# Five edits to a two-layer graph network: the sort's operands in PSUM, one-hots on ScalarE, more routing buffers, no second residual array, result sums on TensorE

## The chip, the cores and the metric

The kernel runs on one core of a Trainium2 chip. The metric is the device time of one execution in microseconds (us), as the median of several runs. The engines are TensorE (PE, with PEld for its weight loads), VectorE (DVE), ScalarE (ACT), GpSimd (POOL) and SyncE (SP). SBUF and PSUM are the on-chip memories of 128 partitions; PSUM takes the results of matmuls.

## What is computed

A graph network of two layers on 6250 nodes of 256 features and 100000 edges, all in fp32. Cut to what matters:

```python
# layer 0
xn = _layernorm(x)
agg = segment_sum(edge_weight[:, None] * xn[src], dst, N)         # GNN
x = x + relu(agg @ W + b) + linear_attention(xn)                  # 8 heads
x = x + expert(argmax(router(_layernorm(x))))                     # 32 experts, top 1
# layer 1
xn = _layernorm(x)
h = (xn @ W).reshape(n, 4, 64)
e = leaky_relu((a_l * h).sum(-1)[src] + (a_r * h).sum(-1)[dst])   # row = src, col = dst
att = exp(e - segment_max(e, src)[src]) / segment_sum(...)[src]
x = x + segment_sum(att * h[dst], src) + galerkin_attention(xn)   # 8 heads
xn = _layernorm(x)
vals, idx = top_k(xn @ gate_w + gate_b, 2)                        # 16 experts, top 2
y = xn + sum(softmax(vals) * expert[idx](xn))
x = x + (y - mean(y)) / sqrt(var(y) + 1e-5) * gamma + beta
```

The edges come sorted by `dst`. Layer 1 needs them sorted by `src`, so the kernel sorts 131072 keys itself.

## The kernel before

Nodes are taken in 49 tiles (NT) of 128, a node a partition. The program is one stream of stages; the times are those of the profiled execution.

**Layer 0, edge loop (126 to 1376 us, L825 to L850).** 196 groups (QA) of four tiles of 128 edges. For each tile POOL issues an indirect DMA that gathers 128 rows (`gather`, L300, `xg<-xw_d,idx`, 782 in all), DVE builds a weighted one-hot matrix S (L836), and PE multiplies it with the rows into the PSUM tile `ps` (L839, four tiles added up; one matmul is two records in the profile). `ps` has three buffers of [128, 256] fp32. Two DVE additions per group (L842) put it where its nodes lie in `agg`. `xg` has six buffers. Between the groups two generators are advanced by a list of due points (L844): `beside`, the linear attention of layer 0, in 99 steps from group 0 to 116, its first half the k and v of each tile (kv steps), its second half the queries and outputs (q steps); and `order`, the sort, its part 1 in 55 steps from group 4 to 116 and its part 2 in 98 steps from group 116 to 192. The scheduler may move these instructions from where they are written; it hasn't a schedule written out by hand here.

**The sort (`edge_order`, L497 to L607).** A bitonic sort of [128, 1024] keys. One step is two DVE instructions, a minimum (L526) and a maximum (L527) of two halves. Part 1 (`step`) sorts within a partition, SBUF to SBUF in the tile `o_x`. Then `banks()` runs `beside` to its end and opens a PSUM pool, since part 2 needs PE transposes (`turned`, L563). After a transpose the keys stand in PSUM (`o_t`); ACT copies one half to SBUF (`o_e`, L588, or `o_z`, L598), and DVE compares PSUM with SBUF. All the other steps of part 2 compare SBUF with SBUF.

**Layer 0 routing and experts, and rows of layer 1 (1376 to 1843).** The routing (`dispatch`, L345 to L495) serves both layers. For groups of `bt` tiles, `logits` makes the layernorm into `xn` and the router's logits, and `put` chooses experts, finds the places of the tokens and scatters the rows (POOL, L442, `f_xs<-xn,d_pi`). The logits of the next group are written ahead of the `put` of the present one.

**Layer 1, attention loop (1843 to 3143).** 25 chunks of up to 32 tiles of edges, in an order written out by hand (`manual_schedule`, L1556 to L1573), three chunks in flight: `loads`; `weigh` (DVE scans for the running maximum, and ACT's exponentials, L1474); `own_part`; `gain` (rows times weights, L1515; a copy by ACT, L1517; one-hots S, L1520; matmuls, L1525); `rows_to` (32 gathers, L300, `h<-h_d,idx`); `own_logits`. The last makes, in steps of eight tiles, a transposed one-hot ST: the row numbers, broadcast from DRAM, are compared with the partition's number in place (DVE, L1378, 128x1024), and PE multiplies with it (L1383).

**Layer 1 routing (3156 to 3380).** `dispatch` in groups of four tiles, with `finals` (L1872) in front: it reads the layer's input `xs1_d` into `xl`, adds the attention, and stores the sum as `xs2_d`.

**Layer 1 experts (3380 to 3782).** PE is busy 398 of 402 us. Beside it `with_beta` (L1914) loads `xs2_d` in seven pieces, adds beta and stores it again. The biases `b2` lie in the memory of `acc`, which is no longer needed.

**Tail (3782 to 3892, L2004 to L2018).** Seven groups of seven tiles: load the two expert results `xc` and `yg` and the residual `xe`, add the two (DVE, L2011), layernorm (L119 statistics, L124 normalisation), times gamma (L2014), plus `xe` (L2015), store.

Of the kernel before, what the change touches and what calls it, by code (L numbers as in the profile page):

```python
# [8 lines left out]
F32 = mybir.dt.float32  # L9
# [11 lines left out]
P = 128  # L21
# [5 lines left out]
CH = 7  # L27
# [25 lines left out]
def gps_kernel(ctx, tc, x, src, dst, edge_weight, g0_W, g0_b, m0_WqT, m0_WkvT, m0_WpT, m0_bp,  # L53
# [12 lines left out]
                   allow_small_or_imprecise_dtypes=True)  # L66
    ident = cst.tile([P, P], F32, name="ident")
# [277 lines left out]
    def dispatch(name, fb, fw, pps, ne, nk, bt, rw, rb, ns, xs_d, finals):  # L345
# [19 lines left out]
        def logits(t0):  # L365
            n = min(bt, NT - t0)
            x_ = finals(t0, n)
            xn = [fw.tile([P, bt, rw_], F32, name=f"xn{k}", bufs=3) for k in range(nk)]
            layernorm(fw, x_, xn[0][:, :, :C], n)
            for k in range(nk):  # L370
                if k:
                    nc.scalar.copy(xn[k][:, :n, :C], xn[0][:, :n, :C])
                nc.vector.tensor_copy(xn[k].bitcast(I32)[:, :n, C], ids[:, k, t0:t0 + n])
                if nk == 2:
                    nc.vector.memset(xn[k][:, :, C + 2], 1.0 - k)
            lp = pps.tile([P, bt, ne], F32, name="lp")
            for i in range(n):
                xT = transposed(fw, pps, xn[0][:, i, :C], "xT")
                for c in range(2):
                    nc.tensor.matmul(lp[:, i, :], xT[:, c, :], rw[:, c, :], start=c == 0, stop=c == 1)  # L380
            lg = fw.tile([P, bt, ne], F32, name="lg")
            nc.vector.tensor_tensor(lg[:, :n, :], lp[:, :n, :],
                                    rb[:, None, :].to_broadcast([P, n, ne]), op=OP.add)
            return xn, lg

        def put(t0, xn, lg, turn):
            n = min(bt, NT - t0)
            ti = fw.tile([P, bt, 8], U32, name="ti")
# [59 lines left out]
        held = logits(0)  # L448
        for j, t0 in enumerate(range(0, NT, bt)):
            ahead = logits(t0 + bt) if t0 + bt < NT else None  # L450
            put(t0, *held, j % 2)
            held = ahead
# [44 lines left out]
    def edge_order(pool, tmp, out, banks):  # L497
# [31 lines left out]
        def step(x, h, flip=False):  # L529

            y = tmp.tile([P, SC], F32, name="o_x")
            pairs(*halves(x, h), *halves(y, h), flip)
            return y
# [24 lines left out]

        def turned(x, i):

            p = pps.tile([P, SH], F32, name=f"o_t{i}")
            for b in range(SH // P):
                nc.tensor.transpose(p[:, b * P:(b + 1) * P],  # L563
                                    x[:, i * SH + b * P:i * SH + (b + 1) * P], ident)
            return p

        half = [slice(i * SH, (i + 1) * SH) for i in range(2)]
        for k in range(7):
            y, z = (tmp.tile([P, SC], F32, name="o_x") for _ in range(2))
            t = [None, None]  # L570
            for i in sides:
                if k:
                    pairs(*halves(x[:, half[i]], 1), *halves(z[:, half[i]], 1))
                    signed(z, y, k + 1, half[i])
                else:
                    signed(x, y, k + 1, half[i])
                t[i] = turned(y, i)
            yield

            for j in reversed(range(k + 1)):  # L580
                y = tmp.tile([P, SC], F32, name="o_x")
                for i in sides:
                    v = t[i].rearrange("p (n two h) -> p n two h", two=2, h=1 << j)
                    a, b = v[:, :, 0, :], v[:, :, 1, :]
                    if j == k:
                        e = pool.tile([P, SH // 2], F32, name="o_e", bufs=2)
                        e = e.rearrange("p (n h) -> p n h", h=1 << j)
                        nc.scalar.copy(e, b)  # L588
                        b = e
                    pairs(a, b, *halves(y[:, half[i]], 1 << j))  # L590
                    t[i] = y[:, half[i]]
                yield
# [7 lines left out]
            x = tmp.tile([P, SC], F32, name="o_x")  # L600
            pairs(p[0], e, x[:, half[0]], x[:, half[1]])
            yield
            for j in reversed(range(1, 9)):
                x = step(x, 1 << j)
                yield
        x = step(x, 1)
# [46 lines left out]
    with tc.tile_pool(name="l0", bufs=1) as lp:  # L653
# [87 lines left out]
        with tc.tile_pool(name="g0w", bufs=4) as gw, tc.tile_pool(name="e0", bufs=1) as ep, \  # L741
                tc.tile_pool(name="e0t", bufs=3) as et, \
                tc.tile_pool(name="g0p", bufs=3, space=PSUM) as gps:
# [71 lines left out]
            late = ExitStack()  # L815

            def banks():

                for _ in beside:
                    pass  # L820
                return late.enter_context(tc.tile_pool(name="e0p", bufs=1, space=PSUM))

            order = edge_order(ep, et, srt1, banks)
            due = [0.0, 0.0, 0.0]
            for b in range(QA):  # L825
                if b % 8 == 0:
                    off = group_values(own0, b, DVE, (NT - 1) * C)
                ps = gps.tile([P, C], F32, name="ps")
# [14 lines left out]
                for k, (rest, first, last, steps) in enumerate(  # L843
                        ((beside, 0, 116, 2 * NT + 1), (order, 4, 116, 55), (order, 116, QA - 4, 98))):  # L844
# [193 lines left out]
    xs2_d = tc.dram_tile([P, NT, C], F32, name="xs2_d")  # L1038
# [180 lines left out]
    with tc.tile_pool(name="g1", bufs=1) as gp, tc.tile_pool(name="g1b", bufs=2) as gw:  # L1219
# [7 lines left out]
        with tc.tile_pool(name="g1bp", bufs=1, space=PSUM) as pps:  # L1227
# [123 lines left out]
            def own_logits(t0, n, pen, fr, STs):  # L1351
# [12 lines left out]
                for u in range(0, n, 8):  # L1364
# [5 lines left out]
                    for k in range(2):  # L1370
# [3 lines left out]
                        else:  # L1374
# [3 lines left out]
                    nc.vector.tensor_scalar(ST[:, :m * P], ST[:, :m * P], pcol, None,  # L1378
                                            op0=OP.is_equal)
# [450 lines left out]
    def expert_pairs(ne, nk, hid, w1_d, b1_d, w2_d, b2_d, rw_d, rb_d, ns, xs_d, ys_d):  # L1830
# [3 lines left out]
        with ExitStack() as ctx1:  # L1834
# [8 lines left out]
            with tc.tile_pool(name="f1w", bufs=1) as wp_:  # L1843
# [10 lines left out]
                with tc.tile_pool(name="f1a", bufs=2) as fw, tc.tile_pool(name="f1b", bufs=1) as fb, \  # L1854
# [17 lines left out]
                    def finals(t0, n):  # L1872
# [18 lines left out]
                        nc.vector.tensor_add(xl[:, :n, :], xl[:, :n, :], accv[:, t0:t0 + n, :C])  # L1891
                        nc.sync.dma_start(xs2_d[:, t0:t0 + n, :], xl[:, :n, :])
# [3 lines left out]
                        return xl[:, :n, :]  # L1896
# [9 lines left out]
                with tc.tile_pool(name="f1x", bufs=1) as fb, tc.tile_pool(name="f1v", bufs=2) as fv, \  # L1906
                        tc.tile_pool(name="f1q", bufs=2, space=PSUM) as pps:
                    b2 = acc[:, :ne * C]
# [4 lines left out]
                    def with_beta(t0):  # L1913
                        xb = fb.tile([P, CH, C], F32, name="xb")  # L1914
                        nc.sync.dma_start(xb, xs2_d[:, t0:t0 + CH, :])
                        yield
                        nc.vector.tensor_tensor(xb, xb, bet[:, None, :].to_broadcast([P, CH, C]),
                                                op=OP.add)
                        yield
                        nc.sync.dma_start(xs2_d[:, t0:t0 + CH, :], xb)  # L1920
# [83 lines left out]
            with tc.tile_pool(name="f1f", bufs=2) as fw:  # L2004
                for t0 in range(0, NT, CH):
                    xc, yg = (fw.tile([P, CH, C], F32, name=q, bufs=3) for q in ("xc", "yg"))
                    for k, q in enumerate((xc, yg)):
                        results(q, ys_d, k, t0, CH)
                    xe = fw.tile([P, CH, C], F32, name="xe", bufs=3)
                    nc.sync.dma_start(xe, xs2_d[:, t0:t0 + CH, :])  # L2010
                    nc.vector.tensor_add(xc, xc, yg)  # L2011
                    yn = fw.tile([P, CH, C], F32, name="yn")
                    layernorm(fw, xc, yn, CH)
                    nc.vector.tensor_tensor(yn, yn, gam[:, None, :].to_broadcast([P, CH, C]), op=OP.mult)  # L2014
                    nc.vector.tensor_tensor(yn, yn, xe, op=OP.add)  # L2015
                    for t in range(t0, t0 + CH):
                        r = rows(t)
                        nc.sync.dma_start(out[t * P:t * P + r, :], yn[:r, t - t0, :])  # L2018

# [44 lines left out]
```

## Time and profile before

| | us |
|---|---|
| median of 7 runs | 3878.09 |
| lowest and highest | 3855.33, 3942.61 |
| profiled execution, own time | 3893.87 |
| span of its trace | 3892.1 |
| edge loop of layer 0 | 126 to 1376 |
| attention loop of layer 1 | 1843 to 3143 |
| tail | 3782 to 3892 |
| busy: PE, DVE, POOL, ACT | 2313.2, 2220.1, 1929.7, 658.1 |

The mean granted clock of TensorE was 0.77 of full speed. A line of the profile names a line of the kernel, an engine, an operation, the tile written and the tiles read (buffer numbers left out); then come the shape, a count, the busy time with the mean duration in ns, and the engine's idle time just before such instructions, with what ended it. "issue" is idle time that the profile ties to no wait, "remote" is idle time that it puts down to something outside of the core's recorded work. The end of a matmul is modelled. A window's busy time says how full an engine is; whether it sets the pace is read from the waits.

### The profile page before, as it was taken

The page shows a single profiled execution, that of the slowest core. Times are in us where ns is not written, and L with a number is a line of the kernel's source. Part 1 is how long each engine was busy: PE and PEld are TensorE (multiplying, and loading weights), DVE is VectorE, ACT ScalarE, POOL GpSimd, SP SyncE. Part 2 cuts the span into 40 slices and gives each one's busy share as a digit, 9 for nine tenths or more (in the row PEclk, how much of TensorE's full clock was granted, in tenths as well). Part 3 has the DMA queues.
Part 4 walks back from the last instruction along what each step waited for, and adds up shares of the span by engine and source line. Part 5 has one row for each costly group of instructions (what it writes and reads, how often), then busy time and mean ns, then how long its engine had stood idle before and what let it go on. Part 6 is the DMA issues. An engine that isn't in the chain of part 4 may idle for free. (4 is left out here: it accounts for less than half of the span.)

```text
span 3892.1 us, 40378 instructions
## 1 busy us (share of the span) xinstructions
PE 2313.2 (59%) x10353; PEld 1767.2 (45%) x10353; DVE 2220.1 (57%) x6266; ACT 658.1 (17%) x1774; POOL 1929.7 (50%) x1895
## 2 busy tenths in 40 slices
PE   5567767776544644766344544356655455499990
PEld 4344555655432443655123332234433255499980
DVE  5255654444664673555356666568775666344448
ACT  2111211110000011322001111001110113244430
POOL 0466765446776723610656565556666405422220
PEclk9888888777776755977667777777777766699995
DMA  6633333222333334456544444345444237577757
GB/s 198 181 104 106 111 101 90 79 83 85 88 89 92 89 75 122 137 178 189 169 129 126 117 139 120 105 129 166 145 143 138 79 127 250 161 246 252 253 172 262
DMA packets 323375, 547.50 MB, mean 141 GB/s; under 512 B 83882, under 2 KB 208531, under 8 KB 322996
## 3 DMA queue, kind: packets, MB, share of 16 engines
q1 hardware_dynamic: 224556, 285.05, 23.2%
q0 software_dynamic: 91104, 245.32, 21.5%
q10 hardware_dynamic: 7464, 14.32, 1.2%
q8 instruction: 93, 1.52, 0.2%
q14 instruction: 158, 1.29, 0.1%
HBM read 431.21 MB, written 116.99 MB: 141 GB/s over the span
## 5 line engine op out<-in xcount | busy, mean ns | idle before, releaser
L300 POOL DMA_INDIRECT h<-h_d,idx x782 | 780.0, 997 | 632.2 <-issue 413.1
L300 POOL DMA_INDIRECT xg<-xw_d,idx x782 | 801.1, 1024 | 554.2 <-issue 209.7
L1525 PE MATMUL ps<-h,S 128*128 128x260 f32 x1564 | 447.5, 449 | 614.0 <-DVE S L1520 392.3
L1525 PEld LDWEIGHTS ps<-h,S 128*128 128x128 f32 x1564 | 348.5, 227 | 724.1 <-DVE S L1520 413.6
L839 PE MATMUL ps<-xg,S 128*128 128x256 f32 x1564 | 469.2, 447 | 232.8 <-DVE S L836 137.1
L839 PEld LDWEIGHTS ps<-xg,S 128*128 128x128 f32 x1564 | 338.2, 228 | 330.6 <-DVE S L836 150.1
L326 POOL DMA_INDIRECT f_ys<-y,xt x175 | 184.8, 1056 | 376.8 <-DVE y L1979 273.4
L842 DVE SCALAR_TENSOR_TENSOR acc<-ps,in,acc 128x256 f32 x392 | 188.1, 480 | 298.6 <-remote 166.1
L1515 DVE TENSOR_TENSOR h<-h,exi 128x2048 f32<-128x2048 f32 x98 | 223.0, 2275 | 64.1 <-ACT exi L1474 54.1
L442 POOL DMA_INDIRECT f_xs<-xn,d_pi x147 | 152.0, 1034 | 204.3 <-DVE d_pi L437 58.9
L836 DVE TENSOR_SCALAR S<-iota,lo,wt 128x128 f32<-128x128 f32 x782 | 239.6, 353 | 0.1
L1958 PE MATMUL hT<-xTt,w 128*128 128x128 f32 x1712 | 210.2, 276 | 0.3 <-ACT xTt L133 0.3
L1383 PE MATMUL p<-ST,hw 128*32 128x512 f32 x392 | 178.2, 603 | 41.1 <-DMA ST<-lob_d 16.3
L1974 PE MATMUL y<-w,h 128*128 x856 | 202.1, 379 | 0.0
L1958 PEld LDWEIGHTS hT<-xTt,w 128*128 128x128 f32 x1712 | 201.3, 193 | 0.6 <-ACT xTt L133 0.5
L1966 DVE TENSOR_SCALAR h<-hT,b1T 128x128 f32<-128x128 f32 x214 | 75.1, 351 | 211.3 <-issue 117.6
L1974 PEld LDWEIGHTS y<-w,h 128*128 128x128 f32 x856 | 154.6, 190 | 16.7
L1520 DVE TENSOR_TENSOR S<-exi,lo 128x1024 f32<-128x1024 f32 x98 | 118.9, 1213 | 61.0 <-ACT h L1517 48.3
L1474 ACT ACT_TABLE_LOAD x24 | 30.8, 1283 | 608.5 <-DVE z L1471 455.5
L1383 PEld LDWEIGHTS p<-ST,hw 128*32 128x32 f32 x392 | 41.4, 111 | 161.8 <-issue 132.1
L131 PE MATMUL tr<-ident,xt 128*128 128x128 f32 x350 | 70.7, 287 | 65.6 <-DMA xt<-f_xs 65.6
L139 PE MATMUL pr<-wp,aT 128*128 128x256 f32 x196 | 65.9, 468 | 70.5 <-ACT aT L133 65.4
(347 smaller groups left out, 3987.6 us busy)
## 6 DMA issues: line engine op xcount, KB each, us to landing
w<-in_L_ffn_w SPq DMA_DIRECT2D x123, 512.0 KB
ST<-lob_d SPq DMA_DIRECT2D x97, 512.0 KB
xt<-f_xs SPq DMA_DIRECT2D x107, 129.5 KB
xnT<-xT SPq DMA_DIRECT2D x98, 128.0 KB
xT<-xnT SPq DMA_DIRECT2D x98, 128.0 KB
xg<-xw_d,idx POOLq DMA_INDIRECT x782
h<-h_d,idx POOLq DMA_INDIRECT x782
xt<-f_xs SPq DMA_DIRECT2D x68, 128.5 KB
```

The source lines that it names most:

```text
L300: nc.gpsimd.indirect_dma_start(out=o, out_offset=None, in_=tab, in_offset=bass.IndirectOffsetOnAxis(ap=idx, axis=0))
L326: st = nc.gpsimd.indirect_dma_start(out=ys_d, in_=y, in_offset=None, out_offset=bass.IndirectOffsetOnAxis(ap=xt.bitcast(I32)[:, C:C + 1], ...
L442: st = nc.gpsimd.indirect_dma_start(out=xs_d, in_=xn[k][:r, i, :], in_offset=None, out_offset=bass.IndirectOffsetOnAxis(ap=pi[:r, t, k:k + ...
L836: nc.vector.tensor_scalar(S[:, i, :], iota, lo0[:, t:t + 1], wt0[:, t:t + 1], op0=OP.is_equal, op1=OP.mult)
L839: nc.tensor.matmul(ps, S[:, i, :], xg[:, i, :], start=i == 0, stop=i == n - 1)
L842: nc.vector.scalar_tensor_tensor(a, ps, m[:, b:b + 1], a, op0=OP.mult, op1=OP.add)
L1383: nc.tensor.matmul(p4[:, :w], hw[:, i, :], ST[:, j * P:j * P + w], start=i == 0, stop=i == nj - 1)
L1515: nc.vector.tensor_tensor(v, v, ex[:, u:u + m, :, None].to_broadcast([P, m, 4, 64]), op=OP.mult)
L1520: nc.vector.tensor_tensor(S[:, :m, :], iop[:, None, :].to_broadcast([P, m, P]), lo1[:, t0 + u:t0 + u + m, None].to_broadcast([P, m, P]), o ...
L1525: nc.tensor.matmul(ps, S[:, i, :], h8[:, i, :], start=i == 0, stop=i == m - 1)
L1958: nc.tensor.matmul(hT[:, f, :], w1[:, c, f * P:(f + 1) * P], xT[:, c, :], start=c == 0, stop=c == 1)
L1974: nc.tensor.matmul(yp, h[:, f, :], w2e[:, f * C:(f + 1) * C], start=f == 0, stop=f == nf - 1)
```

## The change

1. Sort. In part 1 ACT copies half of the keys into a PSUM tile `o_b`, and DVE compares SBUF with PSUM. In part 2 the steps write into PSUM (`o_p`, two banks of 2 KiB in each of two buffers), ACT copies one half back to SBUF (`apart`), and DVE compares PSUM with SBUF. To have the PSUM for it, two groups of the edge loop share one tile `pair` of [128, 2, 256] fp32 (2 KiB), in two buffers. The due points move: `beside` and part 1 to group 110, part 2 to groups 110 to 184.
2. The one-hot ST: two ACT instructions in place, Square(x - p) and Relu(1 - x), for DVE's comparison.
3. `dispatch`: written with two groups held. The written order of `logits` and `put` is the one of before (logits 0, logits 1, put 0, logits 2, put 1, and so on). `xn` has 2 + nk buffers (four in layer 1, three in layer 0, as before), `lg` three for two, and the node ids are copied into `xn` in `put`.
4. `finals` of layer 1 leaves its sum in `acc` and stores nothing; `with_beta` adds beta there in 7 steps for 21; `b2` gets memory of its own, 16 KB a partition.
5. Tail: nine groups (3, 4, five of 7, 4, 3), four buffers of `xc` and `yg`, no `xe`; the sum of the two results on PE with an identity matrix, into PSUM; statistics from PSUM; normalisation on ACT; gamma and the addition of `acc` on DVE.

The core of the diff:

```diff
@@ dispatch
-            xn = [fw.tile([P, bt, rw_], F32, name=f"xn{k}", bufs=3) for k in range(nk)]
+            xn = [fw.tile([P, bt, rw_], F32, name=f"xn{k}", bufs=2 + nk) for k in range(nk)]
...
-            lg = fw.tile([P, bt, ne], F32, name="lg")
+            lg = fw.tile([P, bt, ne], F32, name="lg", bufs=3)
...
-        held = logits(0)
+        held = [logits(0), logits(bt)]
         for j, t0 in enumerate(range(0, NT, bt)):
-            ahead = logits(t0 + bt) if t0 + bt < NT else None
-            put(t0, *held, j % 2)
-            held = ahead
+            put(t0, *held.pop(0), j % 2)
+            if t0 + 2 * bt < NT:
+                held.append(logits(t0 + 2 * bt))
@@ edge_order
         def step(x, h, flip=False):
+            a, b = halves(x, h)
+            e = one.tile([P, SC // 2], F32, name="o_b").rearrange("p (n h) -> p n h", h=h)
+            nc.scalar.copy(e, b)
             y = tmp.tile([P, SC], F32, name="o_x")
-            pairs(*halves(x, h), *halves(y, h), flip)
+            pairs(a, e, *halves(y, h), flip)
             return y
...
+        def bank():
+            return pps.tile([P, SC], F32, name="o_p", bufs=2)
+        def apart(x, h):
+            n = x.shape[-1] // 2
+            a, b = halves(x, h)
+            e = pool.tile([P, SH], F32, name="o_h", bufs=3)
+            e = e[:, :n].rearrange("p (n h) -> p n h", h=h)
+            nc.scalar.copy(e, b)
+            return a, e
...
             for j in reversed(range(k + 1)):
...
+                y = bank() if j else tmp.tile([P, SC], F32, name="o_x")
                 for i in sides:
...
+                    pairs(*ready[i], *halves(y[:, half[i]], 1 << j))
+                    if j:
+                        ready[i] = apart(y[:, half[i]], 1 << (j - 1))
                 yield
...
+            for j in reversed(range(1, 9)):
+                two = apart(x, 1 << j)
+                yield
+                x = bank()
+                pairs(*two, *halves(x, 1 << j))
@@ edge loop
-                ps = gps.tile([P, C], F32, name="ps")
+                if b % 2 == 0:
+                    pair = gps.tile([P, 2, C], F32, name="ps")
+                ps = pair[:, b % 2, :]
...
-                        ((beside, 0, 116, 2 * NT + 1), (order, 4, 116, 55), (order, 116, QA - 4, 98))):
+                        ((beside, 0, 110, 2 * NT + 1), (order, 4, 110, 55), (order, 110, QA - 12, 98))):
@@ own_logits
-                    nc.vector.tensor_scalar(ST[:, :m * P], ST[:, :m * P], pcol, None,
-                                            op0=OP.is_equal)
+                    nc.scalar.activation(ST[:, :m * P], ST[:, :m * P], AF.Square, bias=npcol)
+                    nc.scalar.activation(ST[:, :m * P], ST[:, :m * P], AF.Relu, bias=ones[:, 0:1],
+                                         scale=-1.0)
@@ finals, with_beta
-                        nc.vector.tensor_add(xl[:, :n, :], xl[:, :n, :], accv[:, t0:t0 + n, :C])
-                        nc.sync.dma_start(xs2_d[:, t0:t0 + n, :], xl[:, :n, :])
+                        x_ = accv[:, t0:t0 + n, :C]
+                        nc.vector.tensor_add(x_, xl[:, :n, :], x_)
...
-                    b2 = acc[:, :ne * C]
+                    b2 = fb.tile([P, ne * C], F32, name="b2")
@@ tail
+                for n in (3, 4, CH, CH, CH, CH, CH, 4, 3):
...
+                    for i in range(n):
+                        for k, q in enumerate((xc, yg)):
+                            nc.tensor.matmul(ys[:, i, :], ident, q[:, i, :], start=k == 0, stop=k == 1)
+                    for i in range(n):
+                        nc.vector.bn_stats(st[:, i, :], ys[:, i, :])
...
+                        nc.scalar.activation(yn[:, i, :], ys[:, i, :], AF.Identity,
+                                             bias=rs[:, 1, i:i + 1], scale=rs[:, 0, i:i + 1])
...
+                    nc.vector.tensor_tensor(yv, yv, accv[:, t0:t0 + n, :C], op=OP.add)
```

## The prediction, made before the changed kernel was run

> **What bounds the kernel now.** I read the windows of the stages first, because the whole page (PE 59%, DVE 57%, POOL 50% busy) names no engine. After the window's length come PE, PEld, DVE, ACT and POOL busy with their counts, the granted clock, the DMA share and GB/s.
>
> ```profile
> 126.00:530.00 404.00, 257.78 (x937) 174.55 (x936) 205.76 (x571) 61.65 (x201) 278.91 (x272) 0.82 0.40 115
> 530.00:935.00 405.00, 315.57 (x1384) 239.40 (x1384) 183.69 (x579) 60.85 (x186) 210.62 (x220) 0.81 0.29 85
> 935.00:1376.00 441.00, 214.83 (x722) 160.69 (x720) 273.03 (x731) 8.94 (x20) 311.53 (x291) 0.76 0.30 89
> 1843.00:3143.00 1300.00, 638.63 (x2128) 409.62 (x2128) 843.80 (x2039) 137.10 (x340) 780.01 (x782) 0.74 0.44 128
> 3380.00:3782.00 402.00, 398.07 (x2763) 370.78 (x2764) 181.94 (x429) 161.06 (x426) 112.97 (x104) 0.99 0.73 239
> 3782.00:3893.00 111.00, 4.03 (x22) 3.27 (x20) 81.84 (x184) 4.12 (x10) 2.95 (x3) 0.54 0.66 232
> ```
>
> Rows 1 to 3 are the layer-0 edge loop, row 4 the attention loop, row 5 the last experts (PE alone, untouched by the change), row 6 the tail (DVE alone). ACT is idle in all the touched stages but the routing: whatever goes to it has room. Then the groups (count | busy us, mean ns | idle before, releasers):
>
> ```profile
> L300 POOL DMA_INDIRECT xg<-xw_d,idx x782 | 801.1, 1024 | 554.2 <-issue 209.7 <-PE ps L839 137.9 <-DMA f_xs<-zero 125.3
> L300 POOL DMA_INDIRECT h<-h_d,idx x782 | 780.0, 997 | 632.2 <-issue 413.1 <-DMA lo<-lo_d 169.2 <-ACT sd L1271 26.1
> ...
> L1378 DVE TENSOR_SCALAR ST<-ST,pcol 128x1024 f32<-128x1024 f32 x97 | 72.8, 750 | 8.4 <-issue 4.5 <-DMA ST<-lob_d 4.0
> L526 DVE TENSOR_TENSOR o_x<-o_x 128x512 f32<-128x512 f32 x103 | 70.5, 685 | 0.5
> ...
> L372 ACT COPY xn<-xn 128x1024 f32<-128x1024 f32 x12 | 12.6, 1051 | 4.4 <-DVE xn L124 4.4
> ...
> L526 DVE TENSOR_TENSOR o_x<-o_t,o_z 128x512 f32<-128x512 f32 x7 | 4.8, 684 | 0.0
> ...
> L598 ACT COPY o_z<-o_t 128x512 f32<-128x512 f32 x7 | 4.1, 585 | 104.6 <-PE o_t L563 62.3 <-PE ps L839 23.0 <-DVE acc L842 19.3
> ```
>
> A gather by itself takes 946 ns (the median of both kinds) and its issue gap 307 ns: 782 x 1.253 = 980 us is POOL's floor in each loop, against some 1230 and 1300 us. A compare takes DVE 685 ns from SBUF and 684 ns with PSUM operands. In the timeline the difference is in the gathers beside it: 1132 ns beside L526 and 1230 beside L527 from SBUF, 946 beside the forms with a PSUM operand, 1473 beside L1378. Last, the waits inside single stages: first what holds the gathers at 530:935, then the matmuls at 935:1376, then ScalarE in the attention loop.
>
> ```profile
> POOL xg L300 <- PE ps L839: 114.1, 31, 8.1
> ```
>
> ```profile
> PEld ps L839 <- DVE S L836: 150.1, 31, 26.0
> ```
>
> ```profile
> ACT L1474 <- DVE z L1471: 455.5, 16, 39.1
> ```
>
> Each line has waiter, releaser, total, times and the longest one. So the edge loop has three regimes: gathers set the pace to 530, PE at 78% beside the attention's q steps to 935, DVE with the second sort part to 1376. That the attention loop follows DVE is less sure: its chunks of 32 gathers take 46.5 to 61 us where POOL's floor is 40.1.
>
> **1. Sort and PSUM pairs (edge loop): -30 us.** *Removed:* gather stretching. Excess over 946 ns is 22 us at 126:530 (272 gathers), 3 us at 530:935, 36 us at 935:1376. The compares' own time stays (685 against 684), and each now needs an ACT copy: 55 in part 1, some 90 in part 2, 0.585 us each, 85 us beside 131 us of ACT work in 1250 us. A copy precedes its compare by a scheduled step, about 3.5 us. *Moved:* `beside` and part 1 end at group 110, not 116; part 2 has groups 110 to 184, not 116 to 192. In the kv regime, where POOL paces, three groups fewer at 404/68 = 5.9 us take 18, and 13 of the 22 us of stretching lies there: -31. In the q regime three fewer groups take PE 3 x 2.7 us (the eight matmul records of one, 336 ns each in the timeline) = 8, and bank waits, below, give back 15: +7. Part 2 gains six groups at POOL's 5.0 us (+30), loses 36 of stretching and 8 of the sort's tail, since the last compare now ends at 1373, 17 us after the last gather's 1355.5, and will end before it: -14. That is -38; 8 for bank waits outside the q regime make it **-30**. Bounds: -60 (all 61 us of stretching on the path) and +40 (none on it, every group moved in at its full price plus bank waits).
>
> *The pair:* two groups share 2 KiB of PSUM where each had a tile of its own. Engines that share a PSUM tile are already ordered here even when both read: L1520 waits 48.3 us for ACT's L1517 copy although both only read `exi`. The nearest row for the price is how often a second group's first matmul began before the first group's two additions ended: 12 of 29 pairs at 530:935, 15.5 us in all, 13 of 29 early and 17 of 39 late, 90 and 36 us with PE's own late completions in them. I take 15 there and 8 elsewhere, since S of a group queues on DVE behind the additions of the one before anyway. The Trainium skill, "PSUM - Partial Sum Buffer" (section on bank collisions), speaks against the change: TensorE and another engine must not touch a bank at once, even at disjoint columns. By it every pair would wait in turn; no run here shows a collision.
>
> **2. One-hots of layer 1: -45 us.** *Removed:* 98 x 0.75 us on DVE. In the timeline a step of own_logits takes 1.08 us, and its two short instructions alone 0.47: 0.61 x 98 = 60 us, 2.4 per chunk of 32 gathers. *Added:* 196 ACT instructions of 128x1024, at L372's 1.05 us some 206 us, 8.2 per chunk. They are issued after the chunk's last L1517 copy and before the exponentials, where ACT now waits 28.6 us for z at 2319:2348; cost nothing there. If the cover failed, 25 x 8.2 = 205 us. *Next late:* the gathers. L1410 already waits 38.2 us for h in all, so a fast chunk (46.5 us against 40.1 of POOL) gives less than 2.4; for the stretched ones POOL gains 40 us (997-946, x782), nearly all beside L1378. With 2.4 for sixteen stretched chunks and 0.8 for nine fast ones: **-45**; bounds -80 (DVE's 60 and half of POOL's) and 0 (slow stretches set the pace, POOL "issue" 413 us).
>
> **3. Routing, f1: -15 us.** The order of emission stays L0 L1 P0 L2 P1; what changes is a fourth `xn` buffer, a third `lg`, and the id copy L373 that goes to `put`. It is the wait of that copy for a scatter of the same buffer that lies on the path. Chain of waits, window 3150:3385:
>
> ```profile
> 3207.97 10.24 DMA f_xs<-xn,d_pi
> ...
> 3250.06 5.17 DMA f_xs<-xn,d_pi
> ...
> 3367.39 7.80 DMA f_xs<-xn,d_pi
> ```
>
> They are 23 us; the last drains the stage and stays, so 15 go. In finals the store of xs2 goes too, on SP's queue, which the scatters don't use. Bounds -35 (all L373 waits) and +5 (L373, 162 ns x24, now in front of top-k). f0 keeps three buffers: 0. The b2 load (2 MB) moves from 3205 to about 3375, into a stage start at DMA share 0.9 to 1.0: **+3** (0 to +6). with_beta goes from 21 steps to 7 with no DMA: under 400 us of PE work, 0.
>
> **4. Tail: -28 us.** Seven groups of 7 tiles now cost DVE 2.02 (sum) + 7 x 0.57 (statistics) + 7 x 0.41 (L124) + 2 x 2.02 = 12 us each, 82 in all. The sum goes to PE, L124 to ACT (49 x 0.51, L1949's row, 25 us beside). Left: 4.0 + 0.3 + 4.0 = 8 us, 54 in all: **-28**. The first group of 3 tiles lands about 3 us sooner and the last one of 3 stores less: I leave this against the drains of nine groups. Bounds -38 and 0. PE does 49 x 4 matmul records of 128x256; the expert stage runs 16 such in 3.62 us, 226 ns each at 0.99: 44 us, hidden. The window's clock is 0.54, with PE idle: at that rate 81 us, and PE would be the bound, gain 0. The skill, "TensorE: Matmul & The Clock Gate" (section "What's actually happening"), has half rate by default and full after some 3.4 us of work; it would be 44 to 81 us by how the groups leave gaps.
>
> **Sum:** -30 - 45 - 15 + 3 - 28 = -115. The profiled execution took 3893.87 (span 3892.1): 3779. The median of the seven runs is 3878.09, 0.996 of it: **3763**.
>
> **Rivals.**
> *A, slower: the shared bank serialises PE and DVE.* PE's second group waits for both additions (0.96 us), behind which DVE has S (1.4) and a pair of compares (1.4) queued: 1.2 to 4 us for each of the 98 pairs, 118 to 390 us, if POOL's six buffers run dry as they do at 530:935. Without the edge gain the rest is -85, so it decides from 85 + 19 = 104 us, or 1.1 us per pair on the path. At 2.2 us: -85 + 216 = +131, 4009 us. For: 114 us of POOL waiting for PE. Against: 15.5 us of overlap in the q regime. 0.14.
> *B, no change: edge gain eaten and one more cover gone.* Bank waits at 85 us cancel parts 2 to 4: 3878. 0.08.
> *C, smaller: the tail at half clock, gathers setting layer 1.* -30 - 10 - 15 + 3 - 0 = -52: 3826. 0.23. For: clock 0.54, POOL's issue gaps. Against: DVE 65% busy in the loop with every chain through it.
> *D, the words aren't the change:* "two groups ahead" alters no order; only the buffers count. This is in the sum; if they do nothing either, +15: 3778.
>
> **How the numbers follow.** The forecast with D has 0.55, C 0.23: faster 0.78, same 0.08, slower 0.14. 0.5%, 19 us, is about what a measurement of this kernel tells from none. Favourable ends (30, 35, 20, 3, 10) add in squares to 51: 3712, set to 3705. Unfavourable (70, 45, 20, 3, 28) to 90: 3853; to reach into B, 3868. Left out: A and some of B, 0.18.
>
> **To look for after.** Gathers of xg and h at mean 950 to 965; no excess beside L526/L527; POOL waiting on PE at 530:935 no more than 130 us; last compare before the last gather; chunks 2 us shorter and ACT L1474 still waiting on z; three waits on f_xs down to one; tail of 83 us with PE below 60. Wrong if PE waits on L842 for tens of us, if ACT's one-hots come last before L1383 or L1474, or PE's clock in the tail stays near 0.5.

## The result

The changed kernel took 3890.26 us (median of 30 runs, 3862.34 to 3925.27), the kernel before 3882.99 us (median of 72, 3816.26 to 3973.13). The ratio is 1.0087, with a 95% interval of 1.0065 to 1.0109; it compares undisturbed runs alone and so lies above the ratio of the medians, and of the two profiled executions that of before is a disturbed one, so that the differences between stages below lean in favour of the change. Forecast were 3763 us. The change lost a little where a clear gain was expected.

The later runs fell on several chips, and these are of two kinds for this program: on three the kernel before takes 3445 to 3449 us, on the others 3799 to 3916. The result was measured on the slower kind, called slow chips below, the others fast chips. Each chip was used at one time only, so what belongs to a chip and what to its state at that time are not told apart. On a fast chip the same change gains 3.2%.

The stages, from first and last instructions in the traces (us). The last column sets a run of the changed kernel (`g1_after`) against runs that keep the stage as before: `g4_undo_onehots` from the same chip for the attention loop, `f3_both` from another fast chip for the others.

| stage | before | after | difference | forecast | difference on fast chips |
|---|---|---|---|---|---|
| edge loop: first gather to last addition | 1238.8 | 1230.8 | -8.0 | -30 | -47.2 |
| layer 0 routing, experts, rows | 478.2 | 479.5 | +1.3 | 0 | |
| attention: first gather to first `mix` matmul | 1326.3 | 1346.3 | +20.0 | -45 | -41.8 |
| layer 1 routing to first expert matmul | 215.1 | 225.4 | +10.3 | -12 | -13.6 |
| experts, first to last `hT` matmul (L1958, L1979) | 397.8 | 398.0 | +0.2 | 0 | |
| last `hT` matmul to the end of the span | 109.5 | 97.3 | -12.2 | -28 | -13.2 |

These sum to +11.6, and the spans differ by 12.0. On fast chips the four parts make -116, the medians differ by 110, and the forecast sum was -115. That the sums agree is in part luck: the edge loop gains 17 us more than forecast and the tail 15 less. On the kind of chip that the forecast was made on, every term is wrong. The experiments ask why.

The windows of the changed kernel, columns as in the prediction:

```profile
126.00:530.00 404.00, 277.97 (x989) 188.60 (x990) 201.61 (x567) 87.61 (x253) 261.51 (x272) 0.83 0.40 116
530.00:935.00 405.00, 312.71 (x1360) 236.96 (x1358) 203.55 (x613) 72.06 (x203) 220.04 (x232) 0.81 0.30 88
935.00:1370.00 435.00, 233.38 (x692) 169.43 (x692) 263.55 (x703) 56.47 (x121) 264.76 (x281) 0.71 0.29 86
1837.00:3165.00 1328.00, 632.73 (x2139) 396.92 (x2140) 787.85 (x1951) 350.57 (x538) 742.59 (x782) 0.74 0.42 125
...
3806.00:3904.00 98.00, 58.59 (x220) 46.53 (x218) 54.63 (x143) 27.88 (x61) 2.95 (x3) 0.81 0.61 198
```

In the attention loop DVE has 56 us less to do than before (788 for 844), POOL 37 less, ACT 213 more, and the stretch is longer. In the tail DVE is busy 54.6 us, just the 54 that were worked out, and yet the tail gains 12 and not 28. The groups:

```profile
L302 POOL DMA_INDIRECT xg<-xw_d,idx x782 | 746.1, 954 | 596.0 <-issue 210.2 <-PE ps L864 156.7 <-DMA f_xs<-zero 125.6
L302 POOL DMA_INDIRECT h<-h_d,idx x782 | 742.6, 950 | 693.1 <-issue 442.8 <-DMA lo<-lo_d 171.6 <-ACT sd L1295 39.2
...
L1403 ACT ACTIVATE ST<-ST,ones 128x1024 f32<-128x1024 f32 x97 | 111.4, 1148 | 3.2
L1402 ACT ACTIVATE ST<-ST,npcol 128x1024 f32<-128x1024 f32 x97 | 110.1, 1135 | 16.5 <-DMA ST<-lob_d 16.1 <-issue 0.4
L529 DVE TENSOR_TENSOR o_p<-o_p,o_h 128x512 f32<-128x512 f32 x56 | 39.0, 697 | 0.2
```

The local effects are all there: a gather takes 954 and 950 ns for 1024 and 997, a compare the same time as before (697 for 685), a one-hot 2 x 1.14 us on ACT. But the gathers' busy time went down by 55 and 37 us while POOL's idle time ahead of them went up by 42 and 61. In the attention loop none of that time was saved, and in the edge loop little: it became waiting.

Where DVE waits in the attention loop shows in the line of the copies z, at the head of `weigh`. First the kernel before, then the changed one; durations in ns are least, median, longest:

```profile
L1410 DVEq EVENT_SEMAPHORE  x391: 2/50/4681, 1870.4 to 3133.4; - x196
```

```profile
L1435 DVEq EVENT_SEMAPHORE  x391: 4/691/5066, 1857.3 to 3147.0; - x196
L1435 DVE COPY z<-h x98: 189/197/450, 1857.7 to 3147.1; 128x32 f32<-128x32 f32 x97, 128x24 f32<-128x24 f32 x1
...
  DMA h<-h_d,idx: 214.1, 49
```

The 391 EVENT_SEMAPHORE instructions do nothing but wait for the gathers' semaphores, four ahead of each copy. Before, half of them took up to 50 ns; after, half take 691 or more. The idle time is put down to the gathers, 214 us, but the gathers in question had been issued some 20 us earlier (chunk 17: the last at 2772, its copies run 2792 to 2805). Plain DVE instructions behind them stand 0.70 us apart too, though each takes 0.2. So DVE is hardly waiting for data there; its instructions come at 0.7 us each. A chunk (mean of chunks 1 to 23) is split like this; the third column is DVE's wait for the exponentials, up to the first product of rows and weights (L1515, L1540):

| us per chunk | copies z | rest of weigh | wait for exponentials | gain and own_logits | sum |
|---|---|---|---|---|---|
| before | 2.4 | 14.4 | 2.9 | 31.7 | 51.5 |
| after | 11.4 | 13.9 | 1.4 | 25.8 | 52.5 |
| after, fast chip | 5.3 | 8.3 | 1.4 | 25.3 | 40.3 |

The two rows of the changed kernel differ by 12.2 us, of which the copies z and the rest of weigh are 11.7. That TensorE's granted clock is lower on the slow chip (0.774 in the mean, 0.822 on the fast one) does not explain it: the matmuls of `gain` take nearly the same time (434 and 431 ns), and PE's idle time is what differs. First the slow chip, then the fast one:

```profile
L1550 PE MATMUL ps<-h,S 128*128 128x260 f32 x1564 | 424.1, 434 | 610.4 <-issue 417.7 <-DVE S L1545 192.3
```

```profile
L1550 PE MATMUL ps<-h,S 128*128 128x260 f32 x1564 | 419.6, 431 | 371.3 <-DVE S L1545 371.2
```

In the edge loop of the slow chip it is not these steps: none of DVE's waiting instructions there takes 650 to 740 ns. POOL pauses all the same, 81 times for over 1 us (252 us in all; 50 times and 203 us before, once and 11 us on a fast chip), and afterwards DVE, ACT and POOL go on together. Here they do so within 0.3 us, some 4 us after the modelled end of the last matmul ahead:

```profile
278.13 1.88 PE L791 MATMUL kv<-wkv,xT 128*128 128x512 f32 x4
...
283.73 0.48 DVE L867 SCALAR_TENSOR_TENSOR acc<-ps,in,acc 128x256 f32 x1 [6.70 <-remote]
283.96 0.94 POOL L302 DMA_INDIRECT xg<-xw_d,idx  x1 [2.69 <-remote]
283.97 0.38 ACT L777 ACTIVATE elu_lo<-kv 128x256 f32<-128x256 f32 x1 [8.76 <-remote]
```

### The profile page after: what moved, and what is told of

Its sections match the earlier page's. It is cut to its first block, busy times and chain, and to the rows that moved or that the text cites. A ratio compares the mean times of both kernels' runs of the same rounds, so it can differ in the third digit from the quotient of the medians.

```text
span 3904.1 us, 41172 instructions
## 1 busy us (share of the span) xinstructions
PE 2394.8 (61%) x10549; PEld 1814.6 (46%) x10549; DVE 2134.0 (55%) x6130; ACT 977.8 (25%) x2188; POOL 1838.1 (47%) x1895
## 5 line engine op out<-in xcount | busy, mean ns | idle before, releaser
L302 POOL DMA_INDIRECT h<-h_d,idx x782 | 742.6, 950 | 693.1 <-issue 442.8
L302 POOL DMA_INDIRECT xg<-xw_d,idx x782 | 746.1, 954 | 596.0 <-issue 210.2
L1550 PE MATMUL ps<-h,S 128*128 128x260 f32 x1564 | 424.1, 434 | 610.4 <-issue 417.7
L1550 PEld LDWEIGHTS ps<-h,S 128*128 128x128 f32 x1564 | 335.1, 219 | 714.1 <-issue 447.3
L864 PE MATMUL ps<-xg,S 128*128 128x256 f32 x1564 | 501.5, 472 | 233.2 <-DVE S L861 101.9
L864 PEld LDWEIGHTS ps<-xg,S 128*128 128x128 f32 x1564 | 358.8, 242 | 349.5 <-DVE S L861 121.4
L1408 PE MATMUL p<-ST,hw 128*32 128x512 f32 x392 | 193.9, 626 | 91.0 <-issue 70.5
L1540 DVE TENSOR_TENSOR h<-h,exi 128x2048 f32<-128x2048 f32 x98 | 223.0, 2276 | 28.4 <-ACT exi L1499 24.9
L1979 PE MATMUL hT<-xTt,w 128*128 128x128 f32 x1712 | 210.4, 276 | 0.3 <-ACT xTt L135 0.3
L1979 PEld LDWEIGHTS hT<-xTt,w 128*128 128x128 f32 x1712 | 201.4, 193 | 0.6 <-ACT xTt L135 0.5
L1435 DVE COPY z<-h 128x32 f32<-128x32 f32 x98 | 23.2, 237 | 265.2 <-DMA h<-h_d,idx 214.1
L1499 ACT ACTIVATE exi<-z 128x32 f32<-128x32 f32 x98 | 22.1, 226 | 549.2 <-DVE z L1496 487.8
L573 ACT COPY o_h<-o_p 128x512 f32<-128x512 f32 (+1 forms) x112 | 52.9, 479 | 305.9 <-DVE o_p L529 198.4
```

What stands on the lines that cost most here:

```text
L302: nc.gpsimd.indirect_dma_start(out=o, out_offset=None, in_=tab, in_offset=bass.IndirectOffsetOnAxis(ap=idx, axis=0))
L864: nc.tensor.matmul(ps, S[:, i, :], xg[:, i, :], start=i == 0, stop=i == n - 1)
L1408: nc.tensor.matmul(p4[:, :w], hw[:, i, :], ST[:, j * P:j * P + w], start=i == 0, stop=i == nj - 1)
L1540: nc.vector.tensor_tensor(v, v, ex[:, u:u + m, :, None].to_broadcast([P, m, 4, 64]), op=OP.mult)
L1550: nc.tensor.matmul(ps, S[:, i, :], h8[:, i, :], start=i == 0, stop=i == m - 1)
L1979: nc.tensor.matmul(hT[:, f, :], w1[:, c, f * P:(f + 1) * P], xT[:, c, :], start=c == 0, stop=c == 1)
```

## Experiments

Theory at the start: on the measured chip, time that DVE saves at L1378 is taken back at the next stretch of short instructions. Rivals: the prediction's sum; one part that spoils another; later, ScalarE's 196 instructions as the disturbance.

**One part alone, on one slow chip (before 3799.36 us).** Each kernel is the one before with the named hunks of the diff: the sort with its tile `pair` and its due points; the one-hots with `npcol`; `finals`, `with_beta`, `b2` and the tail; the buffers in `dispatch`.

> Part 1 of the change alone: the sort's operands in PSUM, two groups to a PSUM tile, the due points 110 and 184. Theory (the part works but its gain is small, because POOL was not what the stretched compares held up): the first gather to the last addition of the edge loop takes 1231 us for 1239, as in the changed kernel, all stages behind unchanged; total 5 to 15 us faster. Rival (the prediction's sum): 30 us faster. Second rival (the shared bank costs more than the part gains): slower by 10 us or more, with PE waiting for L842's kin.

> Part 2 alone: ScalarE's one-hots in layer 1. Theory (what DVE saves at L1378 is taken back at the next place where DVE runs many short instructions without a long one, the copies z with their 32 waits): attention loop 15 to 25 us longer than before, first gather to last gather 1243 to about 1264, DVE idle ahead of z near 260 us for 53; total 10 to 25 us slower. Rival (the loss of the attention loop came from the position in time or from the other parts): loop 30 to 45 us shorter, total as much faster.

> Parts 4 and 5: the sum left in acc, b2 with memory of its own, result sums on TensorE, ScalarE's normalisation. Theory (a group of the tail is now a chain through DVE, ACT and DVE again that two PSUM buffers don't overlap fully): last expert matmul to the end 98 us for 109, start of the experts 5 us later; total 0 to 8 us faster. Rival (the prediction): 25 us faster.

> Part 3 alone: fourth xn buffer and third lg buffer in layer 1's routing, id copy in put. Theory (the waits for scatters go, the chain finds the next one): first scatter to last scatter 165 us for 170, total within 8 us of before. Rival (the prediction): 15 us faster.

Measured: e1 3798.75 us, ratio 0.9999 (0.9945 to 1.0052); e2 3891.98, 1.0267 (1.0196 to 1.0338); e3 3777.08, 0.9933 (0.9889 to 0.9976); e4 3795.07, 0.9987 (0.9947 to 1.0027). Of the four only part 2 loses, and much more here than in the result: its attention stage takes 1342 us, those of e1, e3 and e4 1252 to 1277. My 10 to 25 us were too small, since before runs faster on this chip. Part 1 is worth nothing: its edge loop takes 1207.5 us, that of e4, which has the loop of before, 1198.6. The gathers of e4, then of e1:

```profile
L300 POOL DMA_INDIRECT xg<-xw_d,idx x782 | 801.9, 1025 | 512.0 <-issue 213.4 <-DMA f_xs<-zero 123.8 <-PE ps L839 119.3
```

```profile
L300 POOL DMA_INDIRECT xg<-xw_d,idx x782 | 744.7, 952 | 574.0 <-issue 206.6 <-DMA f_xs<-zero 125.6 <-PE ps L862 115.9
```

57 us less in gathers, 62 more idle, and PE's share of that unchanged (119.3 and 115.9): neither a gain nor the shared bank's price.

**ScalarE's work or DVE's place.** One kernel leaves the comparison out on both engines (e6), one keeps DVE as late as before by an idle reduction (e7), one has plain loads of other rows for the gathers (e8), and one is the change without part 2 (e5). The edits, shortened:

```diff
 e6 (on before)
      -  nc.vector.tensor_scalar(ST[:, :m * P], ST[:, :m * P], pcol, None, op0=OP.is_equal)
 e7 (on e2)
      +  nc.vector.tensor_reduce(dum, iota[:, None, :64].to_broadcast([P, 9, 64]), AX.X, OP.max)
         nc.scalar.activation(ST[:, :m * P], ST[:, :m * P], AF.Square, bias=npcol)
 e8 (on e2), f4 (on before)
      -  for i in range(min(8, n - u)): gather(h8[:, i, :], h_d, idx1[:, t:t + 1])
      +  nc.sync.dma_start(h8[:, :m, :], h_d[r0:r0 + m * P, :].rearrange("(i p) c -> p i c", p=P))
```

> The change without part 2: DVE makes the one-hots ST again, all else as in the changed kernel. If part 2 alone carries the loss, this is faster than before by what the others gave by themselves (0.0, 0.7 and 0.1%): ratio 0.985 to 0.997, attention loop as in the kernel before on the same chip (about 1180 us from first to last gather on the chip of the first runs). If the parts disturb one another, 1.00 or more.

> Before, with the comparison L1378 left out (ST stays the row numbers, so the weights of layer 1 differ), and no ScalarE work in its place. Theory (DVE's timing against the gathers decides: without 2.4 us of work per chunk DVE reaches the copies z when the gathers have run for some 13 us without a pause, and there its instructions come one per 0.7 us): as slow as with ScalarE's one-hots, z 10 us or more per chunk, attention loop 1255 to 1270 us, total 2 to 3% above before. Rival (ScalarE's 196 instructions are the disturbance): z 1 to 3 us, loop under 1180 us, total 0 to 2% below before.

> Part 2 alone, with an idle DVE reduction of about 0.73 us in the place of each comparison, so that DVE is as late as before while ScalarE makes the one-hots. Theory (DVE's timing): the loss goes, total within 1% of before, z 1 to 4 us. Rival (ScalarE's work): the loss stays or grows, 2.5% or more.

> Part 2 alone, with the 782 indirect gathers of the attention loop replaced by 98 plain loads of consecutive rows from SyncE's queue (other rows than the edges'). Theory (the slow instructions of DVE come from the gathers beside them): z at 1.1 us and the rest of weigh at about 8 us in every chunk, no semaphore instruction of DVE at 0.7 us, a chunk at 36 to 42 us. Rival (they come from ScalarE or from DVE's own short instructions): z stays near 10 us.

These runs fell on a fast chip (before 3446.73 us): e5 0.9778 (0.9761 to 0.9795), e6 0.9885 (0.9861 to 0.9910), e7 0.9870 (0.9846 to 0.9893), e8 3266.74 us in a single execution. e5 gained more than the parts of the first chip add up to, as part 1 is worth something here (the edge loop takes 1004.8 us, in e6 1053.9). The question itself does not arise: no DVE semaphore instruction between 650 and 740 ns occurs in the attention loop of e5, e6 or e7, where the changed kernel's has 258. e8 gives the price of a chunk that waits for no gather: z 0.4, weigh 7.9, 34.7 us in all.

**The same on another fast chip (before 3449.20).** f1 is e2 again, f2 is e6, f3 is e7.

> Part 2 alone once more, to stand beside its controls on one chip. On the chip of the first runs it cost 2.7%, with z at 10.7 us per chunk; the chip of the second runs ran the kernel before in 3447 us where the first took 3799, and DVE had no instruction at 0.7 us there. If this chip is of the first kind: 1.5 to 3% slower, z 9 to 13 us. If of the second kind: 1 to 2% faster, POOL without pauses at 40 us per chunk.

> L1378 left out and nothing in its place (ST stays the row numbers). Theory (DVE's timing): as f1 on a chip of the first kind, z 9 to 13 us, 1.5 to 3% slower. Rival (ScalarE's instructions disturb DVE): no slower than before. On a chip of the second kind 1% faster, as seen.

> ScalarE's one-hots and DVE kept as late as before by an idle reduction. Theory (DVE's timing): on a chip of the first kind within 1% of before or faster by up to 1% (the exponential's table load, 1.28 us a chunk, now lies ahead of z), z 1 to 4 us. Rival (ScalarE): as f1. On a chip of the second kind 1.3% faster, as seen.

> Before, with the attention loop's gathers replaced by 98 plain loads of consecutive rows. Theory (gathers beside DVE's short instructions make them slow): z 0.4 us, rest of weigh 8 us in every chunk on any chip, a chunk at 35 to 38 us, and L1378's 2.4 us in full on the path (34.7 us with ScalarE's one-hots). Rival: 0.7 us steps remain.

f1 0.9868 (0.9847 to 0.9889), f2 0.9878 (0.9862 to 0.9895), f3 0.9883 (0.9867 to 0.9900). f4, before with the plain loads, took 3361.83 us in a single execution. Part 2 alone gains 43 us here, the forecast's 45. But DVE's saved time is not the reason: f3 keeps DVE's time and gains as much, and f2 leaves ScalarE's work out and gains as much. f4, with DVE's comparison and no gathers, takes 38.5 us a chunk, e8 34.7: of the 3.8 between them 2.5 are the comparison and 1.3 the exponential's table load, which goes from behind z to ahead of it, since ACT, last busy with the one-hots, reaches it early. With gathers in the loop neither counts: f1, f2 and f3 all run at POOL's floor of 40.1 us a chunk (40.35, 40.5 and 40.2), though f2 has the table load where it was and f3 DVE's time. What the three share is that no comparison runs beside the gathers. Both plain loads ran on fast chips, so they say nothing of the slow steps.

**The whole change on a fast chip (before 3445.16).** g2 is the change with the idle reduction of e7, g3 the change without one-hots, g4 the change without part 2 (as e5).

> The changed kernel itself, beside before on one chip. On a chip of the slower kind (before at 3750 us or more): within 1% of before or up to 1.5% slower, z at 10 us or more. On one of the faster kind (before near 3450): the sum of the parts seen there, 0.978 x 0.987 = 0.965, some 3330 us, which is the gain that the prediction named.

> The change with an idle DVE reduction (0.73 us) at the place of each comparison. Theory (on the slower kind DVE's place against the gathers decides): 1.5 to 3% faster than g1 there, z 1 to 4 us. Rival (ScalarE's work): as g1 or slower. On the faster kind within 0.4% of g1.

> The change with the one-hots left out on both engines (ST stays the row numbers). Theory (DVE's place): as g1 on the slower kind, z 10 us or more. Rival (ScalarE's work): 1.5% or more faster than g1. On the faster kind within 0.4% of g1.

> The change without part 2 once more. On the slower kind 0.3 to 1.5% faster than before, and 1.5 to 3% faster than g1, if part 2 alone carries the loss. On the faster kind 2.2% faster than before and 1.3% slower than g1.

g1 3334.88, 0.9681 (0.9656 to 0.9707); g2 3330.04, 0.9667 (0.9641 to 0.9693); g3 3336.35, 0.9688 (0.9661 to 0.9714); g4 3369.79, 0.9775 (0.9749 to 0.9801). The parts add up there. The gathers of the attention loop in g4, which compares on DVE, and in g1:

```profile
L300 POOL DMA_INDIRECT h<-h_d,idx x782 | 784.3, 1003 | 408.3 <-issue 226.3 <-DMA lo<-lo_d 170.3 <-PE ps L1547 6.4
```

```profile
L302 POOL DMA_INDIRECT h<-h_d,idx x782 | 745.7, 954 | 405.4 <-issue 222.7 <-DMA lo<-lo_d 167.5 <-PE ps L1550 7.3
```

Neither has a pause, the idle time is the same, and the gathers differ by 38.6 us where the loops differ by 41.8. So on a fast chip part 2 gains by the gathers that are no longer stretched beside the comparison. POOL's waits in g1, over the attention loop, and then the edge loop's gathers:

```profile
POOL h L302 <- issue: 222.1, 729, 0.3
```

```profile
L302 POOL DMA_INDIRECT xg<-xw_d,idx x782 | 746.1, 954 | 375.3 <-issue 222.1 <-DMA f_xs<-zero 126.7 <-PE ps L864 20.1
```

No gather waits longer than the 0.3 us issue gap: 782 in a row. On the slow chip the same kernel has this, with 43 pauses of 297 us in all:

```profile
POOL h L302 <- issue: 442.8, 757, 19.1
```

**The two kernels that tell, on slow chips (before 3916.17, then 3905.54).** h1 is e6, h2 is g2.

> Before without L1378 and without ScalarE's one-hots (ST stays the row numbers). On a chip of the slower kind (before at 3750 us or more): by DVE's timing 1.5 to 3% slower than before, z 9 to 13 us per chunk; by ScalarE's work 0 to 2% faster, z 1 to 3 us. On one of the faster kind 1.2% faster, as seen twice, and the question stays open.

> The change with an idle DVE reduction (0.73 us) at the place of each comparison. On a chip of the slower kind (before at 3750 us or more): by DVE's place against the gathers 0.5 to 2.5% faster than before, where the change was 0.9% slower, and z 1 to 4 us per chunk; if the place of a few microseconds isn't what decides, 0.5 to 1.5% slower and z near 10 us. On one of the faster kind 3.3% faster, as seen.

h1 took 3953.10, ratio 1.0120 (0.9987 to 1.0254), which is not told apart from equal. It has less work than before on DVE and none added on ACT, and it is no faster; its copies z take 10.2 us per chunk. So the slow pattern comes without ScalarE's instructions too. The line of z in h1:

```profile
L1408 DVEq EVENT_SEMAPHORE  x391: 3/689/7076, 1865.2 to 3199.0; - x196
```

h2 took 3907.60, ratio 1.0035 (0.9990 to 1.0080), with z at 8.8 us per chunk. I expected 1 to 4 us and a gain: putting DVE's 0.73 us back does not restore before's pattern. So my theory falls in its simple form. That DVE comes 2.4 us a chunk earlier is not what decides.

What the slow traces do show is where the slow steps begin. I took each run of gathers with no pause between them, and the first of two successive DVE steps of 0.7 or 1.4 us in it: in the changed kernel it comes 14.6 us and 50 DVE records into the run (medians of 22 runs of gathers, 11.2 to 16.3 us), in h1 some 15 us and 50 records, in h2 17 and 56. It is no fixed time: in before and e1 it comes 17 to 37 us into a run or not at all, and in the first run of each only after some 67 us. On fast chips, in runs of 782 gathers, no waiting instruction of DVE takes 650 to 740 ns, against 258 in the changed kernel's loop on the slow chip. Two patterns follow. In one a chunk's gathers start some 4 us (1 to 13) before the next copies z; `weigh` is over before the steps slow down, the steps of 0.7 us fall beside instructions of 2.3 us and cost nothing, and a chunk takes 39 to 48 us (most chunks of e1 and e4 from the seventh on, chunks 14 to 19 of before). In the other 24 gathers start 13 us before z (17 in h2), `weigh` falls into the slow steps, POOL then pauses some 5 us, issues the last 8 and pauses again; a chunk takes 50 to 52, at times 60. The changed kernel, e2, h1 and h2 stay in the second to the end. What keeps them there stays open: all four have no DVE instruction that writes ST, but no run changed that wait alone. That PE is starved as DVE is, and releases the buffers of the last 8 gathers late, is argued, from PE's 417.7 us of "issue" above (214.5 in before) and from one sign: these gathers and the four loads of ST, which wait for different matmuls, start within 2 us of each other, 15 to 24 us after the modelled ends of those matmuls.

## Why the prediction was wrong, by its own steps

**What bounds the kernel.** I saw POOL's "issue" 413.1 us in the attention loop, where 782 gaps of 0.307 make 240, and left the other 173 as "slow stretches" at the edge of a range. The step that failed is there: time taken off gathers and DVE was counted as time off the path. On the slow chips POOL stood still in both loops, and what was taken off its work came back as pauses. In the attention loop before has 31 pauses of over 1 us, 234 us in all; g4, with the same loop on a fast chip, has none and takes 1082 us for 1326. In this loop a chunk takes its length (11.7 of the 12.2 us above) from how fast instructions come to DVE, and perhaps to PE, which no edit of the change speeds up. What holds the edge loop up on the slow chips stays open.

**Part 1, -30 forecast, -8 measured, 0 for the part alone.** The stretching went as forecast (a gather takes 954 ns); that POOL's work set the pace did not hold: 55 us less of it came with 50 us more of pauses. On a fast chip it holds: idle time ahead of the gathers is equal (371.0 in f1, 375.3 in g1), and the loop gains 47. Rival A, the bank, is refuted on both kinds: POOL's waits for PE at 530:935 went from 114.1 to 91.7 us, over the whole loop e1 has as many of them as e4, and g1 has 20.1 for f1's 16.3.

**Part 2, -45 forecast, +20 measured.** The bound of the range at 0 was wrong: nothing in the trace excluded a loss, and my cover, ScalarE's idle time, was the wrong thing to look at; ACT did have the room (549 us of waiting ahead of L1499). What the sum counted as DVE's gain came back in the copies z: 2.4 us a chunk before, 11.4 after. On a fast chip the gain is the term that the prediction named second, the gathers' 40 us of stretching beside L1378 (38.6 measured, of 41.8); DVE's 2.4 us a chunk gave nothing there, as f3 shows, so that 42 for 45 is the right number from the wrong half of the sum.

**Part 3 and b2, -12 forecast, +10 measured**, -14 on a fast chip. The waits for scatters went as said (those of L373's copy, 34.6 us before, are gone). Each part alone left this stage within 3 us of before's on a slow chip, part 3 too (217.2 in e4), so the loss comes with the combination (222.8 in h2); its cause was not tested.

**Part 4, the tail: -28 forecast, -12 measured on both kinds.** Here the mechanism was right and the term was mis-sized. DVE's work fell by 27 us, but the sum let it run without a gap, and it is now one link of a chain PE, DVE, ACT, DVE. (The items of the sum add up to 12.9 us a group before and 8.3 after, 90 and 58 in all, not 82 and 54; so that DVE's 54 were met is in part luck.) After, in the tail:

```profile
DVE st L2041 <- PE ys L2039: 24.0, 7, 14.4
...
PE ys L2039 <- ACT yn L2050: 14.9, 6, 4.7
...
DVE yn L2053 <- ACT yn L2050: 7.6, 5, 2.8
```

PE waits for ACT to leave one of two PSUM buffers, DVE for PE and for ACT: beyond the first wait of 14.4 us these are 9.6 and 7.6, about the 16 that are missing. The earlier start did not come either: the first statistics begin 18.8 us after the last `hT` matmul, the first sum of before 18.0. The first sums wait behind a slow PE:

```profile
3820.00 1.19 PE L2039 MATMUL ys<-xc,ident 128*128 128x256 f32 x2 [9.72 <-DMA xc<-f_ys]
...
3824.58 0.94 PE L2039 MATMUL ys<-yg,ident 128*128 128x256 f32 x2
3825.36 0.59 PE L2039 MATMUL ys<-xc,ident 128*128 128x256 f32 x2
```

A pair of records takes 0.94 to 1.22 us for 5.4 us and mostly 0.59 from then on; the granted clock is 0.51 up to 3825.4 and 1.00 in the ten microseconds behind it. The half rate that part 4's bound of 0 rested on is real but lasts these 5.4 us, and the window's clock is 0.81.

The Trainium skill, "TensorE: Matmul & The Clock Gate" (section "What's actually happening"), has half rate by default and full rate after some 3.4 us of sustained work. This trace agrees in kind; its 5.4 us are longer.

**Rivals.** D held: no instruction order of the routing changed. C named the right place, issue gaps that set layer 1's pace, and gave it a gain of 10 us where there was a loss of 20. B's total, 3878, is the nearest, but by luck: the bank waits that it is made of did not occur.

**A better version.** On fast chips g2 and g1 are the best (0.967 and 0.968, not told apart). On slow chips e3 alone is faster than before beyond its interval, by 0.7%. The change without part 2 was run on fast chips only.

## What to carry to other kernels

Idle time that ends on nothing ("issue") and exceeds the engine's own gap times its count can be a bound by itself; here work removed beside it turned into more of it. When a bound of a cost is put at zero because an engine is free, ask what limits the engine that is relieved: after part 2 it was not its work. An edit can also pay through another engine: on fast chips DVE's comparison cost what it stretched the gathers beside it. A gain on one chip, or forecast for it, says little where instructions come slowly on another: compare a stage's fastest and slowest chunks in one trace, which before showed here (40.6 and 61.3 us for the same work), and ask what the longest wait for before costing an edit.

## What the runs showed of the hardware

The chips used here differ by 10 to 14% on this program (3445 to 3449 us against 3799 to 3916), with equal gathers (954 and 950 ns in the changed kernel on a slow chip, 954 on a fast one) and equal expert stages (398 us). The difference lies in the stages with indirect DMAs: for the changed kernel 224 us in the edge loop (1230.8 against 1006.9) and 306 in the attention loop (1346.3 against 1040.5), of 578 in all. In the attention loop on the slow chips DVE's instructions, those that only wait for a semaphore included, come 0.70 us apart once gathers have been issued for a time without a pause, 15 us in the changed kernel and 17 to 37 in before, and at 0.02 to 0.05 us again after it. What differs between the chips, and whether it stays with a chip, was not found.

A gather takes 1003 ns in the mean with DVE's comparison in the loop (g4) and 954 without it (g1), and on the fast chips, where the gathers follow each other without a pause, the 38.6 us that this makes for 782 of them are nearly all that the loop gains (41.8).
